# A two-layer graph attention network: column-split sums in layer 2, weights ahead of the rows, few in-edges first

## The chip, the cores and the metric

The kernel runs on one core of a Trainium2 chip. The metric is the device time of one execution in microseconds (us), and lower is better. Three executions of the kernel before took 6455.11, 6468.38 and 6469.05 us; the median is 6468.38.

## The reference, cut to what matters

There are N = 10000 nodes with 768 features each, and 170000 edges: 80000 random pairs in both directions and a self loop for each node; the reference then adds a second self loop. The edges come sorted by their target. Two graph attention (GAT) layers follow each other, each with a layer norm and a residual product, and a layer norm without scale ends the whole:

```python
def gat_conv(x, ei, W, a_src, a_dst, bias, heads, out_ch):
    xl = (x @ W).reshape(n, heads, out_ch)
    e = leaky_relu(alpha_src[src] + alpha_dst[dst], 0.2)   # alpha = sum of xl * a, per node and head
    alpha = softmax of e over the edges of one target      # with + 1e-16 in the divisor
    return segment_sum(xl[src] * alpha[:, :, None], dst) + bias

h1 = relu(layer_norm(gat_conv(x, heads=4, out_ch=256))) + x @ Wr1 + br1     # 768 -> 1024
h  = layer_norm(gat_conv(h1, heads=1, out_ch=768)) + h1 @ Wr2 + br2         # 1024 -> 768
out = layernorm(x + h)
```

All numbers are float32.

## The kernel before, in words

**Stages.** The first stage (to about 955 us of the span) computes `x @ W1` for 79 tiles of 128 nodes and writes `table1`, one row of 1032 numbers (4128 bytes) a node: 1024 features, then four source and four target logits. In the same time it sorts the nodes by their number of in-edges, most first, into `order` (79 columns of 128 nodes) and builds `slots`: for the tile t of the sorted order, `SLOTS[t]` columns of row numbers, one for the node itself and one for each in-edge a node of this tile can have, filled up with a row of zeros whose logits are a large negative number. `SLOTS` comes from `slot_counts`, at build time, from the numbers of nodes and edges alone: 42 for the first tile, then 28, 27 and so on down to 11, 1470 in all. If the input's degrees don't fit these counts, another, general path runs.

**Gathers and ring.** In both layers a tile's rows come one slot at a time: an indirect DMA, issued by GpSimd (POOL), fetches for each of 128 nodes the row of one in-edge into a slot of a ring in SBUF, which `Ring` holds; 28 slots of 1032 columns in layer 1, 40 of 770 in layer 2. `ring.fetch` (line 388) issues gathers as far ahead as the ring allows: after the row of slot q is used, that of q + 28 or q + 40 is asked for. So the ring's next gather waits for the engine that used the slot last.

**Layer 1, per tile** (`ordered_layer1`, from line 581). `logits` (409 to 417) forms the edge weights from the last columns of all the tile's rows, `normalised` (423 to 426) divides them by their sum. The first two rows (`ON_PE1`) are summed by TensorE (PE), which multiplies the row by a diagonal matrix of its weights; ScalarE (ACT) makes the diagonals. The other rows go to VectorE (DVE) in `weigh`: one row in three as four `scalar_tensor_tensor` of 256 columns (line 439: multiply by the head's weight and add), two in three are first multiplied in place on ScalarE (line 433) and then added by one operation of 1024 columns (line 435). The sum `acc` is in PSUM. While the rows of tile t are summed, tile t - 1 is finished: `deviation` and `scaled` make the layer norm, line 635 applies the relu and adds `x @ Wr1`, `columns` transposes h on TensorE, and a product with `W2` gives the row of `table2` that is scattered to memory by an indirect DMA on POOL; the transposed h is stored to `h1_d`. The schedule is written out by hand (`manual_schedule`): each engine takes its instructions in the order of the code, and `events` places the pieces of tile t - 1 after a given row of tile t. All products and the transposes of layer 1 take their PSUM tiles from `ps_big`, two buffers of two banks each, which lives through the whole kernel; `ps_acc` has two more.

**Layer 2, per tile** (`ordered_layer2`, from line 683). The same ring with rows of 768 columns and two logits. All rows are summed by VectorE, one `scalar_tensor_tensor` of 768 columns each (line 439), into one PSUM tile of two banks. TensorE computes the residual: line 740 adds x, gathered by POOL, with an identity product, line 742 adds `h1 @ Wr2` from `h1_d`, which SyncE (SP) loads. x and h1 of tile t + 2 are asked for at the end of tile t (line 763). The last layer norm ends on ScalarE (line 733), and POOL scatters the result (line 758).

**The first tile.** The tile of 42 slots has more rows than a ring holds. It goes through `attend_parts`: groups of rows with a running maximum, whose sums are scaled down when the maximum rises. It is the first in both layers, since the nodes of most in-edges come first. All other tiles are whole.

Of the kernel before, what the change touches and what calls it, by code (L numbers as in the profile page):

```python
# [33 lines left out]
P = 128  # L34
# [9 lines left out]
RING2 = 40  # L44
ON_PE1 = 2
# [8 lines left out]
def slot_counts(n_nodes, n_edges):  # L54
# [8 lines left out]
    for t in range(-(-n_nodes // P)):  # L63
        room = t * P if t else 0.002
        k = next((k for k, m in enumerate(tails) if m + 4.0 * math.sqrt(m) * (t > 0) <= room), DEGREES - 3)
        counts.append(min(k + 1, DEGREES - 2))
# [4 lines left out]
def gnn_kernel(ctx, tc, x, x_cols, src, dst, src_col, dst_col, W1, a_src1, a_dst1, b1, g1, be1, Wr1, br1,  # L71
# [13 lines left out]
    FIRST = [sum(SLOTS[:t]) for t in range(NT)]  # L85
# [12 lines left out]
    ps_big = ctx.enter_context(tc.tile_pool(name="ps_big", bufs=2, space=PSUM))  # L98
    ps_tr = None

    @contextmanager
    def psum_for_transposes():

        nonlocal ps_tr
        with tc.tile_pool(name="ps_tr", bufs=2, space=PSUM) as ps_tr:
            yield
# [8 lines left out]
    slots = consts.tile([P, FIRST[-1] + SLOTS[-1]], I32, name="slots")  # L115
# [29 lines left out]
    def product(aT, w, n):  # L145

        k = w.shape[1]
        p = ps_big.tile([P, 2 * BANK], F32, name="big")
        for c in range(0, n, BANK):
            e = min(n, c + BANK)  # L150
            for j in range(k):
                nc.tensor.matmul(p[:, c:e], aT[:, j, :], w[:, j, c:e], start=(j == 0), stop=(j == k - 1))  # L152
        return p
# [226 lines left out]
    class Ring:  # L380
# [6 lines left out]
        def fetch(self, upto):  # L387
            for q in range(self.issued, min(upto, FIRST[-1] + SLOTS[-1])):
# [38 lines left out]

    def weigh(acc, row, e, dh, first=None, shared=False):

        if shared:  # L430
            for h in range(e.shape[1]):
                s = slice(h * dh, (h + 1) * dh)
                nc.scalar.activation(row[:, s], row[:, s], AF.Copy, scale=e[:, h:h + 1])  # L433
# [8 lines left out]
    def attend_parts(small, ring, acc, h_, ad, bias, heads, dh, t):  # L442
# [6 lines left out]
        for lo, hi in zip(cuts, cuts[1:]):  # L449
# [13 lines left out]
            for q in range(lo, hi):  # L463
                weigh(acc, ring.slot(q), e[:, q - lo], dh, shared=heads > 1 and (q - lo) % 3)
# [3 lines left out]
    def deviation(small, a, n):  # L468

        k = -(-n // BANK)  # L470
        st = small.tile([P, k, 6], F32, name="st")
        for j in range(k):
            nc.vector.bn_stats(st[:, j, :], a[:, j * (n // k):(j + 1) * (n // k)])
# [6 lines left out]
    def scaled(to, a, n, mean_and_deviation, g, b):  # L480

        mean, inv = mean_and_deviation
        nc.vector.scalar_tensor_tensor(to, a[:, :n], mean, g, op0=OP.subtract, op1=OP.mult)
# [29 lines left out]
    with tc.tile_pool(name="w1", bufs=1) as w1p, tc.tile_pool(name="l1", bufs=2) as io, \  # L513
            psum_for_transposes(), tc.manual_schedule():
# [65 lines left out]

    def ordered_layer1():
        with tc.tile_pool(name="b1", bufs=1) as pool, tc.tile_pool(name="small1", bufs=2) as small, \
                tc.tile_pool(name="ps_acc1", bufs=2, space=PSUM) as ps_acc, tc.manual_schedule():
            ring = Ring(pool, table1, R1, RING1)
            ring.fetch(RING1)

            def fetch_x(t):
                xt = pool.tile([P, D0], F32, name="xt", bufs=2)
                gather(xt, x[:, :], order[:, t:t + 1])
                return xt  # L590

            xs = {t: fetch_x(t) for t in range(min(2, NT))}
            g1_b, be1_b = (spread(pool, v, n) for v, n in ((g1, "g1"), (be1, "be1")))

            def transposed_x(t):
                to = pool.tile([P, K0, P], F32, name="xT", bufs=2)
                return to, columns(to, xs[t])

            xT, moves = transposed_x(0)
            last = None  # L600
            for t in range(NT + 1):
                live, events = t < NT, []
                whole = live and SLOTS[t] <= ring.size
                n = SLOTS[t] if live else 0
                if live:
                    acc = ps_acc.tile([P, 2 * BANK], F32, name="acc")
                if whole:
                    ad = ring.slot(FIRST[t])[:, C1 + H1:]
                    e, _ = logits(small, ring, FIRST[t], FIRST[t] + n, ad, H1, C1)
                if last:  # L610
                    h, r, mean_rows = last
                    stats = deviation(small, mean_rows, C1)
                if whole:
                    normalised(small, e, H1)

                    diagonals = pool.tile([P, ON_PE1 * H1, P], F32, name="diagonals")
                    for k in range(ON_PE1):
                        for i in range(H1):
                            nc.scalar.activation(diagonals[:, k * H1 + i, :], ident, AF.Copy,  # L619
                                                 scale=e[:, k, i:i + 1])  # L620
                    for k in range(ON_PE1):
                        for i in range(H1):

                            c, d = i * DH1, (i + 1) * DH1
                            nc.tensor.matmul(acc[:, c:d], diagonals[:, k * H1 + i, :],  # L625
                                             ring.slot(FIRST[t] + k)[:, c:d],
                                             start=(k == 0 and c % BANK == 0),
                                             stop=(k == ON_PE1 - 1 and (d % BANK == 0 or d == C1)),
                                             skip_group_check=True)
# [404 lines left out]
```

## Time and profile before

| What | Kernel before |
|---|---|
| median of three executions | 6468.38 us (6455.11 to 6469.05) |
| profiled execution, own time | 6474.16 us |
| its span in the trace | 6472.3 us |
| granted TensorE clock, mean | 0.819 |
| VectorE busy | 5053.9 us (78% of the span) |
| TensorE busy, matmuls / weight loads | 4198.2 us (65%) / 2278.5 us |
| GpSimd busy | 3534.4 us (55%) |
| ScalarE busy | 2688.0 us (42%) |
| moved by DMA | 1666 MB, 257 GB/s in the mean |

An engine's busy time is that of its own instructions, without the time in which it waits for another. Lines such as L439 are line numbers of the kernel. A group of instructions is shown as line, engine, operation, output <- inputs, the shape of each, xcount, then busy time in us, the mean ns of one, and the idle time of the engine ahead of them with what ended it. In a timeline the first number is the time at which a run of instructions of one line starts, the second its length, and the square brackets hold the wait ahead of it.

### The profile page before, as it was taken

What the parts mean: (1) busy time and instruction counts of PE and PEld (TensorE: products, weight loads), DVE (VectorE), ACT (ScalarE), POOL (GpSimd) and SP (SyncE); (2) the same over time, 40 slices, a digit from 0 to 9 for tenths busy, and PEclk for the clock granted to TensorE, in tenths of its full rate; (3) what the DMA queues carried; (4) which work ended last, traced back from release to release, by engine and by line L of the source; (5) the groups of instructions that cost most, each with busy time, mean ns of one, the idle gap of its engine ahead of it and who ended that gap; (6) DMA issues with size and microseconds to landing.
All of it is one profiled execution on the core that took longest, in us unless ns stands there. A gap on an engine that the chain in (4) does not pass through costs nothing. (4 is left out here: it accounts for less than half of the span.)

```text
span 6472.3 us, 48744 instructions
## 1 busy us (share of the span) xinstructions
PE 4198.2 (65%) x11636; PEld 2278.5 (35%) x11636; DVE 5053.9 (78%) x8160; ACT 2688.0 (42%) x6591; POOL 3534.4 (55%) x3582
## 2 busy tenths in 40 slices
PE   8997982556766777778888996333434444445555
PEld 3443431333434444444455553111212222222332
DVE  5861426888888888888888884888878888888888
ACT  3433434666666666667666772011111111111111
POOL 3426534555555555555555553666666666666663
PEclk9999996778888888889899998666667777777777
DMA  4323237888888888888888885888878888888884
GB/s 140 122 76 70 93 106 287 289 293 315 299 301 301 303 304 297 300 295 299 293 299 307 308 312 180 277 281 288 281 272 287 282 280 281 279 286 283 279 291 161
DMA packets 459455, 1666.17 MB, mean 257 GB/s; under 512 B 105739, under 2 KB 109899, under 8 KB 459158
## 3 DMA queue, kind: packets, MB, share of 16 engines
q0 software_dynamic: 362176, 1486.59, 66.6%
q1 hardware_dynamic: 93168, 170.98, 7.8%
q10 hardware_dynamic: 3814, 5.39, 0.3%
q8 instruction: 94, 1.54, 0.1%
q14 instruction: 203, 1.66, 0.1%
HBM read 1516.88 MB, written 146.19 MB: 257 GB/s over the span
## 5 line engine op out<-in xcount | busy, mean ns | idle before, releaser
L364 POOL DMA_INDIRECT ring<-table,slots x2940 | 2789.2, 949 | 2161.4 <-DVE acc L439 889.7
L439 DVE SCALAR_TENSOR_TENSOR acc<-ring,e,acc 128x256 f32<-128x256 f32 (+1 forms) x3248 | 2332.4, 718 | 363.5 <-PE acc L625 201.5
L433 ACT ACTIVATE ring<-ring,e 128x256 f32<-128x256 f32 x3400 | 1390.8, 500 | 0.0
L435 DVE TENSOR_TENSOR acc<-acc,ring 128x1024 f32<-128x1024 f32 x850 | 1048.0, 1233 | 91.9 <-ACT ring L433 2.6
L740 PE MATMUL big<-wr,ident 128*128 128x512 f32 (+1 forms) x316 | 206.7, 745 | 1280.2 <-DMA wr<-in_x_dram,order 633.2
L742 PE MATMUL big<-w,wr 128*128 128x512 f32 (+1 forms) x2528 | 950.4, 531 | 23.1 <-issue 23.0
L625 PE MATMUL acc<-ring,diagonals 128*128 128x256 f32 x1248 | 424.3, 514 | 698.9 <-ACT diagonals L619 586.8
L152 PE MATMUL big<-w,hT 128*128 128x512 f32 (+1 forms) x2528 | 840.2, 490 | 56.8 <-ACT hT L494 56.8
L152 PE MATMUL big<-w,xT 128*128 128x512 f32 x1896 | 833.4, 601 | 55.8 <-DMA xT<-in_x_cols_dram 34.7
L152 PE MATMUL big<-wr,xT 128*128 128x512 f32 x1896 | 829.5, 594 | 0.7 <-ACT xT L494 0.7
L742 PEld LDWEIGHTS big<-w,wr 128*128 128x128 f32 x2528 | 531.3, 210 | 468.1 <-issue 432.6
L477 ACT ACTIVATE sd<-mv,eps 128x1 f32<-128x1 f32 x237 | 69.7, 294 | 1358.1 <-issue 585.4
L152 PEld LDWEIGHTS big<-w,hT 128*128 128x128 f32 x2528 | 471.9, 189 | 411.8 <-issue 289.1
L625 PEld LDWEIGHTS acc<-ring,diagonals 128*128 128x128 f32 x1248 | 326.9, 269 | 782.7 <-ACT diagonals L619 598.2
L152 PEld LDWEIGHTS big<-w,xT 128*128 128x128 f32 x1896 | 363.3, 193 | 522.9 <-issue 501.8
L740 PEld LDWEIGHTS big<-wr,ident 128*128 128x128 f32 x316 | 69.7, 249 | 1349.3 <-issue 449.3
L152 PEld LDWEIGHTS big<-wr,xT 128*128 128x128 f32 x1896 | 360.8, 190 | 423.4 <-issue 417.7
L417 ACT ACT_TABLE_LOAD x156 | 200.1, 1283 | 717.7 <-DVE e L416 636.7
L569 DVE TENSOR_TENSOR scr<-big,as_b 128x1024 f32<-128x1024 f32 x79 | 96.7, 1224 | 441.2 <-ACT row L566 426.3
L574 POOL TENSOR_TENSOR row<-row,none 128x1024 f32<-128x1024 f32 x79 | 187.0, 2368 | 334.9 <-ACT row L566 334.3
L572 ACT ACTIVATE scr<-scr 128x256 f32<-128x256 f32 x632 | 253.4, 402 | 122.2 <-DVE scr L569 118.3
L477 ACT ACT_TABLE_LOAD x157 | 201.4, 1283 | 229.7 <-DVE mv L475 149.5
(146 smaller groups left out, 3359.3 us busy)
## 6 DMA issues: line engine op xcount, KB each, us to landing
ring<-table,slots POOLq DMA_INDIRECT x2940
table<-row SPq DMA_DIRECT2D x79, 516.0 KB
h_d<-hT SPq DMA_DIRECT2D x79, 512.0 KB
wr<-h_d SPq DMA_DIRECT2D x79, 512.0 KB
xT<-in_x_cols_dram SPq DMA_DIRECT2D x79, 384.0 KB
w<-in_W_dram SPq DMA_DIRECT2D x6, 512.0 KB
w<-in_W_dram SPq DMA_DIRECT2D x1, 3072.0 KB
wr<-in_Wr_dram SPq DMA_DIRECT2D x1, 3072.0 KB
```

Of the source, the lines that this page charges most:

```text
L152: nc.tensor.matmul(p[:, c:e], aT[:, j, :], w[:, j, c:e], start=(j == 0), stop=(j == k - 1))
L364: nc.gpsimd.indirect_dma_start(out=to, out_offset=None, in_=table, in_offset=bass.IndirectOffsetOnAxis(ap=index, axis=0), **more)
L417: nc.scalar.activation(e, e, AF.Exp)
L433: nc.scalar.activation(row[:, s], row[:, s], AF.Copy, scale=e[:, h:h + 1])
L435: nc.vector.tensor_add(acc[:, :c], acc[:, :c], row[:, :c])
L439: nc.vector.scalar_tensor_tensor(acc[:, s], row[:, s], e[:, h:h + 1], (acc if first is None else first)[:, s], op0=OP.mult, op1=OP.add)
L477: nc.scalar.activation(sd, mv[:, 1:2], AF.Sqrt, bias=eps)
L572: nc.scalar.activation(m[:, s], m[:, s], AF.Copy, accum_out=row[:, C1 + i * H1 + h:C1 + i * H1 + h + 1])
L574: nc.gpsimd.tensor_add(row[:, :C1], row[:, :C1], b1_b)
L625: nc.tensor.matmul(acc[:, c:d], diagonals[:, k * H1 + i, :], ring.slot(FIRST[t] + k)[:, c:d], start=(k == 0 and c % BANK == 0), stop=(k == ...
L740: nc.tensor.matmul(r[:, c:d], ident, xt[:, c:d], start=True, stop=False)
L742: nc.tensor.matmul(r[:, c:d], hT[:, j, :], wr2[:, j, c:d], start=False, stop=(j == K1 - 1))
```

## The change

1. `slot_counts` takes the spread of a binomial count (the factor `1 - m / n_nodes`) for its margin; the counts are now 42, 28, ... 10, 9, in all 1456.
2. `SLOTS` and `FIRST` are turned around after the first stage and `nodes(t)` reads `order` from its end: tiles with few in-edges come first, that of 42 slots last.
3. Layer 1: `weights_of(t + 1)` makes the weights, the diagonals and TensorE's two rows of the next tile `LEAD` = 3 rows before the end of tile t. ScalarE's multiplies are issued three rows ahead of the row that is added, by `multiplied`. Three of four rows (`SHARE` = 4) are multiplied on ScalarE. The statistics of the layer norm and its square root (line 493 after) stand in front of the tile's multiplied rows. The transposes of x are made in the tile that uses them. The row of `table2` is copied and scattered one tile later, in `store`.
4. Layer 1's PSUM: one tile of `ps_h1` for transposes and the product with `W2`, one of `ps_r1` for `x @ Wr1`, two for the sums.
5. Layer 2: the columns 0 to 511 (`ON_PE2` = 512) are summed by VectorE as before, the columns 512 to 767 by TensorE with a diagonal for each row (`sums`), each in a PSUM tile of one bank of its own; ScalarE makes the diagonals. The bias of TensorE's columns comes by a product with ones. `deviation` and `scaled` take the two tiles as parts; the statistics are taken over three pieces of 256 columns.
6. Layer 2: the next tile's weights are made three rows ahead; x and h1 of the next tile are asked for at the middle row; the product with `br1` is made after the first tile's residual and added at the end of its rows. At the start of each layer the gathers of the first tile stand ahead of the first x, the rest of the ring after it.

The diff, cut; a helper's body that only moved is left out:

```diff
-        k = next((k for k, m in enumerate(tails) if m + 4.0 * math.sqrt(m) * (t > 0) <= room), DEGREES - 3)
+        k = next((k for k, m in enumerate(tails)
+                  if m + 4.0 * math.sqrt(m * (1.0 - m / n_nodes)) * (t > 0) <= room), DEGREES - 3)
...
+    FIRST = [sum(SLOTS[t + 1:]) for t in range(NT)]
...
+    def multiply(row, e, dh):
+        for h in range(e.shape[1]):
+            s = slice(h * dh, (h + 1) * dh)
+            nc.scalar.activation(row[:, s], row[:, s], AF.Copy, scale=e[:, h:h + 1])
...
+    def deviation(small, parts):
+        st = small.tile([P, len(parts), 6], F32, name="st")
+        for j, a in enumerate(parts):
+            nc.vector.bn_stats(st[:, j, :], a)
...
+    def scaled(to, parts, mean_and_deviation, g, b):
...
+        for a in parts:
+            d = c + a.shape[1]
+            nc.vector.scalar_tensor_tensor(to[:, c:d], a, mean, g[:, c:d], op0=OP.subtract, op1=OP.mult)
+            c = d
         nc.vector.reciprocal(inv, inv)
         nc.vector.scalar_tensor_tensor(to, to, inv, b, op0=OP.mult, op1=OP.add)
...
+    SLOTS, FIRST = SLOTS[::-1], FIRST[::-1]
+    def nodes(t):
+        return order[:, NT - 1 - t:NT - t]
...
     def ordered_layer1():
...
+                tc.tile_pool(name="ps_h1", bufs=1, space=PSUM) as ps_big, \
+                tc.tile_pool(name="ps_r1", bufs=1, space=PSUM) as ps_r, tc.manual_schedule():
...
+            def weights_of(t):
+                n = SLOTS[t]
+                e, _ = logits(small, ring, FIRST[t], FIRST[t] + n, ring.slot(FIRST[t])[:, C1 + H1:], H1, C1)
+                yield e
+                normalised(small, e, H1)
+                acc = ps_acc.tile([P, 2 * BANK], F32, name="acc")
...
+                yield acc
+            def shared(k):
+                return (k - ON_PE1) % SHARE > 0
...
+            def store(t):
+                nonlocal full
+                row = pool.tile([P, R2], F32, name="row")
+                nc.scalar.copy(row, full[:, :R2])
+                full = None
+                nc.gpsimd.indirect_dma_start(
+                    out=table2[:, :], out_offset=bass.IndirectOffsetOnAxis(ap=nodes(t), axis=0),
+                    in_=row, in_offset=None)
             for t in range(NT + 1):
...
                 if last:
+                    r, mean_rows = last
+                    stats = deviation(small, pieces(mean_rows[:, :C1], BANK))
+                if full is not None:
+                    store(t - 2)
...
+                    xT = pool.tile([P, K0, P], F32, name="xT")
+                    moves = columns(xT, xs[t])
+                multiplied(ON_PE1 + 2)
                 if last:
+                    h = pool.tile([P, C1], F32, name="h")
+                    scaled(h, [mean_rows[:, :C1]], stats, g1_b, be1_b)
+                    nc.vector.scalar_tensor_tensor(h, h, 0.0, r[:, :C1], op0=OP.max, op1=OP.add)
...
+                    events = [(ON_PE1 + j, move) for j, move in enumerate(columns(hT, h))]
+                if live:
+                    r = product(xT, wr1, C1, ps_r)
+                def to_layer2():
+                    nonlocal full
+                    nc.sync.dma_start(h1_d[t - 1], hT.rearrange("p k n -> p (k n)"))
+                    full = product(hT, w2, R2)
+                if last:
+                    events.append((ON_PE1 + 2, to_layer2))
...
+                for k in range(n if whole else 0):
+                    multiplied(k + 1 + LEAD)
+                    if k >= n - LEAD:
+                        ready += itertools.islice(ahead, 1)
+                    if k >= ON_PE1:
+                        weigh(acc, ring.slot(FIRST[t] + k), e[:, k], DH1, shared=shared(k))
+                    ring.fetch(FIRST[t] + k + 1 + ring.size)
+                    due(k)
...
     def ordered_layer2():
...
+                tc.tile_pool(name="ps_acc2", bufs=2, space=PSUM) as ps_acc, \
+                tc.tile_pool(name="ps_q2", bufs=2, space=PSUM) as ps_big, tc.manual_schedule():
...
+            def sums(t, acc, e):
+                n = SLOTS[t]
+                nc.tensor.matmul(acc, ones, b2_b[0:1, ON_PE2:], start=True, stop=False)
+                for k in range(n):
+                    if k == n // 2:
+                        yield
+                    if k % G == 0:
+                        diagonals = pool.tile([P, G, P], F32, name="diagonals", bufs=2)
+                    nc.scalar.activation(diagonals[:, k % G, :], ident, AF.Copy, scale=e[:, k, :])
+                    nc.tensor.matmul(acc, diagonals[:, k % G, :],
+                                     ring.slot(FIRST[t] + k)[:, ON_PE2:C2], start=False, stop=(k == n - 1))
...
                 if last:
+                    h, r, means = last
+                    stats = deviation(small, [a for m in means for a in pieces(m, C2 - ON_PE2)])
+                    next(tail, None)
+                    scaled(h, means, stats, g2_b, be2_b)
                     nc.vector.tensor_add(h, h, r[:, :C2])
+                    mean, inv = deviation(small, pieces(h, C2 // 2))
                     o = pool.tile([P, C2], F32, name="out")
+                for _ in tail:
+                    pass
...
                 if live:
+                    r = residual(t)
+                    if not t:
+                        q = product(brT, wr2, C2)
...
+                    for k in range(n if whole else 0):
+                        if k >= n - LEAD:
+                            ready += itertools.islice(ahead, 1)
+                        weigh(acc, ring.slot(FIRST[t] + k), e[:, k], ON_PE2, None if k else b2_b)
+                        ring.fetch(FIRST[t] + k + 1 + ring.size)
+                        if last and k == 1:
+                            finish()
+                        if not t and k == n - LEAD:
+                            nc.vector.tensor_add(be2_b, be2_b, q[:, :C2])
+                        if t + 1 < NT and k == n // 2:
+                            ins[t + 1] = fetch_x(t + 1)
...
-                if t + 2 < NT:
-                    ins[t + 2] = fetch_x(t + 2)
```

## The prediction, made before the changed kernel was run

> **What bounds the kernel now.** I read the page's slices first, then the busy time by stage, then the groups by shape, then the timeline of one tile in each layer. The page (busy tenths in 40 slices of 162 us):
>
> ```profile
> PE   8997982556766777778888996333434444445555
> DVE  5861426888888888888888884888878888888888
> PEclk9999996778888888889899998666667777777777
> ```
>
> Slices 1 to 6 are the first product, 7 to 24 are layer 1, from 25 on layer 2. VectorE (DVE) is near 0.87 in both layers and TensorE is not. By stage (columns: stretch, length, then busy us of PE, PEld, DVE, ACT, POOL, granted clock, DMA share, GB/s):
>
> ```profile
> 955.00:1091.00 136.00, 15.73 (x36) 7.42 (x36) 76.99 (x138) 46.97 (x118) 68.31 (x73) 0.54 0.80 293
> 1091.00:3919.00 2828.00, 2144.58 (x6609) 1259.38 (x6610) 2421.89 (x3805) 1919.96 (x4577) 1464.98 (x1553) 0.87 0.85 298
> 3919.00:4103.00 184.00, 81.72 (x240) 45.40 (x239) 81.70 (x122) 22.82 (x52) 83.54 (x87) 0.72 0.67 232
> 4103.00:6440.00 2337.00, 1088.83 (x2772) 586.16 (x2770) 1972.10 (x3072) 338.29 (x462) 1493.79 (x1541) 0.72 0.82 277
> ```
>
> The cuts are where the softmax weights of a tile are ready (line 426): 77 tiles of layer 1 take 2828 us, 77 of layer 2 take 2337. The first stage (955 us) is not touched. The groups by shape give the prices:
>
> ```profile
> L364 POOL DMA_INDIRECT ring<-table,slots x2940 | 2789.2, 949 | 2161.4 <-DVE acc L439 889.7 <-issue 478.9 <-PE acc L625 422.3
> L439 DVE SCALAR_TENSOR_TENSOR acc<-ring,e,acc 128x768 f32<-128x768 f32 x1392 | 1423.2, 1022 | 99.7 <-DVE acc L439 42.8 <-issue 11.3 <-remote 3.1
> L435 DVE TENSOR_TENSOR acc<-acc,ring 128x1024 f32<-128x1024 f32 x850 | 1048.0, 1233 | 91.9 <-ACT ring L433 2.6 <-DVE acc L435 0.9 <-DVE acc L439 0.5
> L439 DVE SCALAR_TENSOR_TENSOR acc<-ring,e,acc 128x256 f32<-128x256 f32 x1856 | 909.2, 490 | 263.9 <-PE acc L625 201.5
> ```
>
> The gathers wait mostly for slots that VectorE has not freed: VectorE leads, the transfers follow. One tile boundary of layer 1 in VectorE's timeline:
>
> ```profile
> 2431.22 1.22 DVE L635 SCALAR_TENSOR_TENSOR h<-h,big 128x1024 f32<-128x1024 f32 x1
> 2435.16 2.06 DVE L439 SCALAR_TENSOR_TENSOR acc<-ring,e,acc 128x256 f32<-128x256 f32 x4 [2.72 <-PE acc L625]
> 2437.33 2.57 DVE L435 TENSOR_TENSOR acc<-acc,ring 128x1024 f32<-128x1024 f32 x2
> ```
>
> VectorE sits 2.72 us until TensorE's two rows are there; the group above adds this up to 201.5. An unmultiplied row costs 2.06 + 0.11 = 2.17, a multiplied one 2.57 / 2 = 1.285. In layer 2 the same timeline has two speeds:
>
> ```profile
> 5197.08 0.21 DVE L475 BATCH_NORM_AGGREGATE mv<-st 128x2 f32<-128x12 f32 x1 [1.74 <-remote]
> 5201.97 1.02 DVE L485 SCALAR_TENSOR_TENSOR wr<-wr,sd,be 128x768 f32<-128x768 f32 x1 [2.40 <-remote]
> 5204.78 0.18 DVE L169 SCALAR_TENSOR_TENSOR e<-e 128x19 f32<-128x19 f32 x1 [0.53 <-DVE e L409]
> 5211.77 16.89 DVE L439 SCALAR_TENSOR_TENSOR acc<-ring,e,acc 128x768 f32<-128x768 f32 x16
> ```
>
> In the last line a row takes 16.89 / 16 = 1.055. In the first three VectorE waits for nothing but itself and starts late. Summed over the stage these pauses are some 300 us, 3.9 a tile; tiles of 19 rows take 27.3 us without and 36 to 37 with them. I can't name their cause. POOL and TensorE in the same tile:
>
> ```profile
> 5214.75 0.95 POOL L364 DMA_INDIRECT ring<-table,slots  x1 [0.30 <-issue]
> 5216.00 0.95 POOL L364 DMA_INDIRECT ring<-table,slots  x1 [0.31 <-DVE acc L439]
> ```
>
> ```profile
> 5208.65 8.63 PE L742 MATMUL big<-w,wr 128*128 128x512 f32 x16
> 5217.55 3.62 PE L742 MATMUL big<-w,wr 128*128 128x256 f32 x16
> ```
>
> A gather comes every 1.25 us at best. A pass of 256 columns takes 0.226 us (3.62 / 16), one of 512 takes 0.43 once warm and 0.86 in the first five microseconds.
>
> **What the Trainium skill says.** "VectorE: DVE Perf Modes", section on the TRN2 errata: a fixed cost per instruction and then a slope by element. The trace agrees: 490 ns at 256 columns, 1022 at 768, so 1.04 ns a column. "DMA: Bandwidth & Descriptors", section "SWDGE vs HWDGE vs iDMA": descriptors of GpSimd's transfers are computed there in software; the trace has 0.95 + 0.30 us for each gather. "TensorE: Matmul & The Clock Gate", Part 1: half clock after idling; the 0.86 and 0.43 agree. "PSUM — Partial Sum Buffer", section on bank collisions: two engines must not be in one bank at once, so TensorE's 256 columns need a bank of their own; no run here shows a collision.
>
> **The change, part by part.** *Layer 1, rows.* Before, 77 tiles have 446 rows by VectorE alone and 817 multiplied on ScalarE: 446 x 2.17 + 817 x 1.285 = 2018, which leaves (2828 - 2018) / 77 = 10.5 a tile. After (three of four rows multiplied, 1456 slots instead of 1470 in each layer) 78 tiles have 344 and 914: 1921. ScalarE gets 914 x 4 x 0.41 = 1499 us of multiplies for 1346, some 28 us a tile with its copies and tables, under VectorE's 32 for 18 rows: hidden, with four to spare.
>
> *Layer 1, weights ahead.* The next tile's weights, diagonals and two TensorE rows are issued with three rows left, so the 2.7 goes: 7.8 a tile, 78 x 7.8 = 608, sum 2529. The square root now stands before the multiplied rows, which costs nothing: ScalarE runs ahead of VectorE. Three things are late next. TensorE needs 10.5 (24 passes at 0.436) + 10.6 (16 at 0.436, 16 at 0.226) + 3.6 (16 at 0.226) + 1.9 for transposes = 26.6 a tile, and now its transposes and the layer 2 product share one PSUM tile; tiles of 9 to 14 rows fall to that floor: +40. The weights want all rows of the next tile three rows earlier in a ring of 28; in the 16 tiles of 22 rows or more VectorE will wait for a gather, between 0 and 5 us each; I take 2.5: +40. The transfers must run at 11.0 MB in 33 us, 333 GB/s, where streaming windows show 340 to 356; between 0 and 1.5 us a tile, I take 0.5: +40. Layer 1's whole tiles: 2650 for 2828 + 23 (last tile).
>
> *Layer 2, columns.* 256 of 768 columns go to TensorE. A row of 512 is half way between 490 and 1022, 756, with its gap 0.79 instead of 1.055; at 19 rows this saves 5.0 of 27.3, and one more statistic and one more piece of the scaling give back 0.4. Average 22.1, with the old pauses 26.0. ScalarE gets 1414 diagonals at 0.386, 7 us a tile where it was idle. TensorE gets 36 passes at 0.226, 8.3, beside the 11.9 of the residual product: 20, hidden under VectorE if warm. A slot is now freed by both engines, but TensorE's share stands at the tile's start. The pace passes to POOL: 1414 x 1.253 + 78 x 2.6 (the x gather and the output scatter) = 1975, 25.3 a tile. The x gather moves to mid-tile, behind n/2 gathers and ahead of the rest, and the h1 load with it: TensorE's waits for x (633 us) had cover, now they go. I take 26.0 + 0.9 where neither covers the other, 26.9 x 78 = 2098 for 2337 + 13.
>
> *Order.* The 42-row tile is now last. Layer 1 starts after 9 gathers: 21 us instead of 136, but the large tile costs 64.6 in rows, 20 in group starts, fading and dividing and 6 for the tile ahead: 90. From layer 1's last row (3942) to layer 2's first whole tile (4103) passed 161, among it 39 of VectorE waiting for a bias and 32 for a product; now 22 (h, product, scatter) + 34 (9 gathers, bias): 56. At the end 57 for the large tile. Last 20 us as before.
>
> Sum: 955 + 21 + 2650 + 90 + 56 + 2098 + 57 + 20 = 5947, against 955 + 136 + 2828 + 23 + 161 + 2337 + 13 + 20 = 6473 (span 6472.3, its own time 6474.2, median 6468.4). Forecast 5950.
>
> **The rivals.** *B, pauses set layer 2's pace.* In a paused stretch VectorE's rows start every 1.40 us, and a 512 column row would too, so the saving is lost there; with POOL running without a break, stretches may grow. For it: pauses come late in long POOL runs and end when the gathers are through. Against: layer 1 has none. Layer 2 stays at 30.3 a tile: 78 x 30.3 = 2363, total 6215. *C, all cover holds:* layer 1 at 2569, layer 2 at POOL's 1975, total 5745. *D, slower:* TensorE becomes layer 2's bound. The new passes wait for a diagonal each; if the clock stays at half, a tile needs 18 x 0.86 + 18 x 0.43 + 37 x 0.43 = 39 us, 3042 in all, total 6890. It decides from 33.5 us a tile, the point where the gains elsewhere are eaten. Against it: layer 1 holds full clock at 19.3 of 20 us busy; for it: layer 2's clock is 0.72 today. That the input no longer fits the smaller slot counts, and the general path runs, I exclude: by the input's own in-degrees every tile of 128 nodes stays within its count.
>
> **How the numbers follow.** Forecast 0.52 (5850 to 6080), B 0.26 (6080 to 6350), C 0.13 (5700 to 5850), D 0.07, no difference 0.02. A run of this kernel tells 0.2% from nothing. Faster by more 0.91, within 0.02, slower 0.07. From 5790 to 6290 the range leaves out D, no difference, the top of B (0.03) and half of C: about 0.19.
>
> **What would show it.** Layer 1: no wait of VectorE for TensorE at line 449 in tiles over 15 rows, 33 to 34 us a tile; if it waits for ring gathers at line 415, the transfers bound it. Layer 2: gathers back to back at 1.25 with VectorE waiting at line 415; rows at 0.79; if rows start every 1.40, B. TensorE near 20 us a tile at a clock above 0.85; if VectorE waits at line 504 or 835 for a square root behind diagonals, D. The middle: layer 2's first tile some 56 us after layer 1's last row. A longer first stage would make the whole working wrong.

## The result and the profile after

On the chip of the record the changed kernel takes 6426.99 us (median of five runs, 6419.05 to 6432.44) and the kernel before 6455.39 us (median of five, the three above among them): a ratio of 0.995, 95% interval 0.9933 to 0.9967. It is faster by half a per cent where 8% was forecast.

The runs were made on several occasions, each on one chip; on some the kernel before took 6447 to 6482 us in all of its runs and on the others 6167 to 6172 us, so I call the first kind *late* and the second *in time*, for a reason that the traces give, and compare times within one kind only; the record is of the late kind, both kernels.

The changed kernel on record by stage; columns: stretch, length, then busy us of TensorE, its weight loads, VectorE, ScalarE and GpSimd, granted clock, DMA share, GB/s. The cuts are the first weights of layer 1, the start of its 42-row tile, the first weights of layer 2, and the start of its 42-row tile.

```profile
981.00:3645.00 2664.00, 2135.27 (x6674) 1238.34 (x6674) 2350.36 (x3504) 2080.63 (x4977) 1534.54 (x1580) 0.91 0.89 322
3645.00:3794.00 149.00, 40.32 (x106) 21.76 (x106) 80.38 (x136) 57.10 (x136) 42.70 (x44) 0.63 0.49 170
3794.00:6346.00 2552.00, 1894.23 (x5834) 1230.24 (x5835) 1614.14 (x3237) 757.04 (x1877) 1526.61 (x1583) 0.83 0.77 261
6346.00:6417.00 71.00, 7.48 (x25) 4.50 (x23) 55.34 (x88) 6.26 (x11) 5.26 (x4) 0.57 0.07 23
```

In layer 1 VectorE is busy 88% of the time (2350 of 2664 us). In layer 2 no engine is: VectorE has 63%, GpSimd 60%, TensorE 74%. The forecast had 2098 us where the third line has 2552. The groups of the same run show where VectorE stands (busy, mean ns, idle time ahead and what ended it):

```profile
L449 DVE SCALAR_TENSOR_TENSOR acc<-ring,e,acc 128x512 f32<-128x512 f32 x1336 | 1008.3, 755 | 39.4
L828 DVE TENSOR_TENSOR wr<-wr,big 128x768 f32<-128x768 f32 x79 | 75.4, 954 | 769.4 <-remote 555.7 <-PE sum L792 204.7 <-issue 8.8
```

A row of 512 columns costs 755 ns, as estimated. The idle time has one place: line 828, the addition of TensorE's residual, stands 769.4 us, 9.9 a tile. VectorE, then the queue of SyncE, GpSimd and ScalarE around one such wait:

```profile
5029.67 1.02 DVE L505 SCALAR_TENSOR_TENSOR wr<-wr,sd,be 128x768 f32<-128x768 f32 x1
5041.18 0.95 DVE L828 TENSOR_TENSOR wr<-wr,big 128x768 f32<-128x768 f32 x1 [10.49 <-remote]
```

```profile
5041.17 0.32 SPq L765 DMA_DIRECT2D wr<-h_d  x1
```

```profile
5036.81 1.03 POOL L871 DMA_INDIRECT out_dram<-out,order  x1 [0.30 <-issue]
5044.80 0.97 POOL L370 DMA_INDIRECT ring<-table,slots  x1 [6.96 <-DVE acc L449]
```

```profile
5041.39 0.40 ACT L791 ACTIVATE diagonals<-ident,e 128x128 f32<-128x128 f32 x1 [10.33 <-remote]
```

VectorE's addition, SyncE's load of h1 and ScalarE's ninth diagonal wait for matmuls that the trace has long behind them: the residual's last one starts at 5029.39, the sixth sum, past the four whose diagonals ScalarE overwrites, at 5032.80. All three go on within 0.22 us, 3.3 us after GpSimd's run of gathers and the scatter ended (5037.84). That is when the last packets of the run land, here at 5041.11: over layer 2 of this run the last packet of a transfer ends 3.2 us after GpSimd's instruction in the median, 2.8 to 3.6 in nine of ten.

What they share is TensorE's semaphore: SyncE's load and ScalarE's diagonal wait for nothing else, and VectorE's step that waits for its own semaphore ahead of the addition was through at 5030.75. The trace also notes when a semaphore was raised (us; the first two lines list the starts of TensorE's matmuls that raise it, by line, the third the times at which it was raised):

```
5017.78 L792  5020.14 L803  5023.57 L803  5026.37 L803  5027.23 L803  5028.10 L803  5028.96 L803  5029.39 L803
5030.02 L785  5030.64 ... 5032.80 L792 (6)  5038.14 L792
5040.93 5040.99 5041.05 5041.11 5041.16 5041.20 5041.24 5041.28 5041.33 5041.37 5041.41 5041.45 5041.50
```

Sixteen matmuls raise it, at least 0.43 us apart; from 5017.74 to 5040.93 no signal is noted, and then thirteen come in 0.57 us (three are missing from the trace). So TensorE had computed; its signals came late, all at once, when the gathers were through. The Trainium skill's "Perfetto Trace Analysis", section "Per-engine timelines", shows for each engine that a profiled instruction ends before its raised semaphore is seen everywhere, and that TensorE's end is an estimate. Here that remainder is 11.4 us for the residual's last matmul (5029.77 to 5041.18) and 8.2 us for the sixth sum (5033.18 to 5041.39).

A tile of layer 2 is then a closed round: VectorE waits at line 828 for the end of GpSimd's run; the first slot of the next tile comes free 3.6 us later (5041.18 to 5044.80); GpSimd issues 20 gathers and scatters at 1.25 us (to 5037.84), and 3.3 us later the addition goes on. 3.6 + 25.1 + 3.3 = 32.0, the time from one addition to the next (5009.14 to 5041.18).

On an occasion in time the same program takes 5926.08 us, beside 6169.19 for the kernel before: 0.961, one run of each, without an interval. Its stages, with the corresponding cuts, and the same group:

```profile
983.00:3636.00 2653.00, 2139.33 (x6675) 1239.21 (x6676) 2350.22 (x3504) 2080.61 (x4977) 1533.57 (x1580) 0.91 0.90 324
3636.00:3785.00 149.00, 38.68 (x106) 21.17 (x106) 80.25 (x134) 57.11 (x136) 41.99 (x45) 0.63 0.49 171
3785.00:5837.00 2052.00, 1733.64 (x5831) 1179.42 (x5832) 1620.05 (x3239) 764.62 (x1877) 1554.20 (x1576) 0.90 0.93 323
```

```profile
L828 DVE TENSOR_TENSOR wr<-wr,big 128x768 f32<-128x768 f32 x79 | 75.4, 954 | 11.4 <-PE big L803 3.5
```

Layer 1 is the same within 11 us. Layer 2 is 500 us shorter, the wait at line 828 is 11.4 us in all instead of 769.4, and GpSimd issues almost without a break. The granted clock of layer 2 is lower on the late occasion (0.83 for 0.90), but that does not explain the wait: in the tile above the residual's matmuls were through 11 us before the addition began. VectorE and GpSimd at one boundary of a tile there:

```profile
5124.26 1.02 DVE L505 SCALAR_TENSOR_TENSOR wr<-wr,sd,be 128x768 f32<-128x768 f32 x1
5125.39 0.95 DVE L828 TENSOR_TENSOR wr<-wr,big 128x768 f32<-128x768 f32 x1
```

```profile
5123.67 0.95 POOL L370 DMA_INDIRECT ring<-table,slots  x1 [0.30 <-issue]
5124.92 1.18 POOL L370 DMA_INDIRECT ring<-table,slots  x1 [0.30 <-PE sum L792]
5126.41 0.95 POOL L370 DMA_INDIRECT ring<-table,slots  x1 [0.30 <-DVE wr L828]
```

### The profile page after: what moved, and what is told of

The parts are those of the page before. It is cut to its first block, busy times and chain, and to the rows that moved or that the text cites. A ratio compares the mean times of both kernels' runs of the same rounds, so it can differ in the third digit from the quotient of the medians.

```text
span 6417.3 us, 57909 instructions
## 1 busy us (share of the span) xinstructions
PE 4943.3 (77%) x14620; PEld 2874.9 (45%) x14620; DVE 4584.9 (71%) x7969; ACT 3257.0 (51%) x8379; POOL 3547.9 (55%) x3554
## 5 line engine op out<-in xcount | busy, mean ns | idle before, releaser
L449 DVE SCALAR_TENSOR_TENSOR acc<-ring,e,acc 128x256 f32<-128x256 f32 (+1 forms) x2760 | 1705.2, 618 | 123.8 <-PE acc L641 37.7
L438 ACT ACTIVATE ring<-ring,e 128x256 f32<-128x256 f32 x3776 | 1532.8, 505 | 0.0
L792 PE MATMUL sum<-ring,diagonals 128*128 128x256 f32 x2828 | 914.5, 477 | 619.5 <-issue 327.7
L445 DVE TENSOR_TENSOR acc<-acc,ring 128x1024 f32<-128x1024 f32 x944 | 1163.0, 1232 | 93.1 <-issue 8.6
L792 PEld LDWEIGHTS sum<-ring,diagonals 128*128 128x128 f32 x2828 | 664.2, 241 | 866.8 <-issue 440.3
L803 PE MATMUL big<-w,wr 128*128 128x512 f32 (+1 forms) x2528 | 850.6, 488 | 29.8 <-issue 29.8
L791 ACT ACTIVATE diagonals<-ident,e 128x128 f32<-128x128 f32 x1414 | 441.9, 387 | 571.8 <-remote 384.8
L641 PE MATMUL acc<-ring,diagonals 128*128 128x256 f32 x1248 | 357.5, 450 | 380.3 <-ACT diagonals L636 346.3
L803 PEld LDWEIGHTS big<-w,wr 128*128 128x128 f32 x2528 | 479.7, 190 | 373.8 <-issue 340.0
L828 DVE TENSOR_TENSOR wr<-wr,big 128x768 f32<-128x768 f32 x79 | 75.4, 954 | 769.4 <-remote 555.7
```

Source lines behind the costliest of these rows:

```text
L445: nc.vector.tensor_add(acc[:, :c], acc[:, :c], row[:, :c])
L449: nc.vector.scalar_tensor_tensor(acc[:, s], row[:, s], e[:, h:h + 1], (acc if first is None else first)[:, s], op0=OP.mult, op1=OP.add)
L641: nc.tensor.matmul(acc[:, c:d], diagonals[:, k * H1 + i, :], ring.slot(FIRST[t] + k)[:, c:d], start=(k == 0 and c % BANK == 0), stop=(k == ...
L791: nc.scalar.activation(diagonals[:, k % G, :], ident, AF.Copy, scale=e[:, k, :])
L792: nc.tensor.matmul(acc, diagonals[:, k % G, :], ring.slot(FIRST[t] + k)[:, ON_PE2:C2], start=False, stop=(k == n - 1))
L803: nc.tensor.matmul(r[:, c:d], hT[:, j, :], wr2[:, j, c:d], start=False, stop=(j == K1 - 1))
```

## The experiments

All edits are made in the changed kernel. *Theory J*: on some occasions the signals of gathers at full rate hold up those of the engines, TensorE's above all. *Theory K*: VectorE waits at line 828 for the end of the run of gathers by the order of the program.

**Columns back on VectorE**, in time first, late second; the sums on TensorE, its diagonals and the second PSUM tile go:

```diff
-                    acc = ps_acc.tile([P, BANK], F32, name="acc")
-                    sum_ = ps_acc.tile([P, BANK], F32, name="sum")[:, :C2 - ON_PE2]
-                    tail = sums(t, sum_, e)
+                    acc = ps_acc.tile([P, 2 * BANK], F32, name="acc")[:, :C2]
...
-                        weigh(acc, ring.slot(FIRST[t] + k), e[:, k], ON_PE2, None if k else b2_b)
+                        weigh(acc, ring.slot(FIRST[t] + k), e[:, k], DH2, None if k else b2_b)
```

> The changed kernel with layer 2's columns put back: all 768 on VectorE, no diagonals and no sums on TensorE. Theory J (TensorE's signals pile up behind those of a run of gathers; the more matmuls TensorE signals, the longer VectorE waits for them at the residual's addition, 10 us a tile now): 27 signals a tile are left of about 47, the wait shrinks and a whole tile of layer 2 takes some 30.3 us, as before, instead of 32.3: about 6250. Rival K (VectorE waits there for the end of POOL's run of gathers, whatever TensorE does): the tile stays at POOL's run and the round trip, 32.3: about 6417.

It took 5954.6 us, with the kernel before at 6172.45: lower than both expectations, because this occasion was in time and I had assumed a late one. Three more edits ran beside it:

> The changed kernel with one small memset on GpSimd after each gather of layer 2, so that a gather comes every 1.5 us or so instead of every 1.25. Theory J: signals no longer pile up, the 10 us wait falls under 2 and GpSimd's 20.4 x 1.5 = 30.6 sets the tile: about 6290. Rival K: the wait lasts until the longer run is through, 20.4 x 1.5 + 6.6 = 37.2 a tile: about 6795.

> The changed kernel with gathers of layer 2 of 616 bytes a row instead of 3080, as many of them; the rows are not those of the reference, the weights neither, and the ring is cleared once (some 30 us). Theory J (it is the number of signals): the wait stays and the tile stays at 31 to 32.3: 6350 to 6450. Rival M (it is the bytes that fill the way into SBUF): the wait goes, GpSimd's 25.5 sets the tile: about 5930.

> The changed kernel without h1 @ Wr2 in the residual of layer 2: only x by the identity, 3 matmuls a tile instead of 27; part of the computation is left out. Theory J: TensorE's signals fall from about 47 to 23 a tile, the wait at the residual's addition falls under 3 us and the tile comes to 26 or 27: about 6000. Rival K: still 32.3, about 6417.

They took 6176.13, 5934.48 and 5948.48 us. Without late signals there was nothing for these three to separate; the kernel before, 283 us under its time on record, was the finding. That is the size of the pauses of "some 300 us" that the prediction read from its trace; no trace of the kernel before was taken in time, so that they are the same 300 us is not shown. The changed and the earlier kernel themselves came next, with the columns once more:

> The changed kernel itself, unedited, beside the three edits of it, because the kernel before took 6172 us on the chip of the first four runs and 6455 to 6469 on the one of the record. Theory J (late signals): if this chip gives the kernel before in 6170, the changed kernel has no 10 us wait at the residual's addition either and takes about 5950 to 6000; if it gives 6460, the wait is there and it takes about 6420. Theory K (the wait is in the order of the program): about 6420 on either chip.

> The kernel before, unedited, for its trace on this chip. Theory J: where it takes 6170, the 300 us in which VectorE waits for nothing but itself in layer 2 are gone, and the rest of its stages stands as on record. Theory K: the pauses are there in any trace.

> Layer 2's columns back on VectorE, on the same chip as the changed kernel: VectorE's rows then set a tile at 26.5, about 5955 on a chip without late signals. Against the changed kernel on the same chip it tells what the columns alone are worth: theory J says nothing or less than 1% without late signals (GpSimd's 25.5 a tile is near), and 150 to 250 us in favour of this kernel with them; K says 150 to 250 us in favour of this kernel on any chip.

The occasion was late: 6457.4 us for the kernel before (median of seven; 6453.34 in its traced run), 6429.92 for the changed kernel (0.9954, 0.9938 to 0.9971), 6236.17 without the columns (0.9653, 0.9636 to 0.9669). The columns alone cost 194 us there. In the trace without them the addition (then line 826) waits 66.7 us in all:

```profile
L826 DVE TENSOR_TENSOR wr<-wr,big 128x768 f32<-128x768 f32 x79 | 75.4, 954 | 66.7 <-remote 44.0 <-PE big L803 8.7 <-PE big L801 6.8
```

The changed kernel was run again:

> The changed kernel once more. If this chip gives the kernel before in about 6170: theory J (late signals, found only on the chip with 6455) says 5950 to 6000 with no long wait at the residual's addition; theory K (order of the program) says about 6420. If it gives it in about 6455, 6420 to 6435 as known.

> The changed kernel with the memset on GpSimd after each gather of layer 2 (a gather every 1.58 us instead of 1.25, 29.3 a tile on the first chip, 6176 in all), on whichever chip this is. On a chip with 6455 for the kernel before: theory J (the signals of a run of gathers at full rate hold up those of TensorE) says that at this rate they don't, the wait at the residual's addition falls under 2 us and the time is 6180 to 6250. Theory K (the wait lasts until the run of gathers is through, at any rate): about 6750.

This occasion was in time, and the two took 5926.08 and 6178.69 us. So the wait is not in the order of the program, and K in that form falls. In time the columns gain little: 0.961 of the kernel before with them, 0.965 without (5954.6 of 6172.45), single runs on two occasions.

**What goes with late signals: gathers of 616 bytes a row, and slower gathers.** The gathers of layer 2 read a fifth of a row, in the same number; the rows and weights are then not the reference's.

```diff
-                gather(self.slot(q), self.table[:, :], slots[:, q:q + 1])
+                gather(self.slot(q)[:, :self.part],
+                       self.table.rearrange("n (a b) -> (n a) b", b=self.part), slots[:, q:q + 1])
...
             ring = Ring(pool, table2, R2, RING2)
+            ring.part = 154
+            nc.vector.memset(ring.rows, 0.0)
```

> The changed kernel with gathers of 616 bytes a row in layer 2 for 3080 (the rows and weights are then not the reference's, and the ring is cleared once). On a chip with 6170 for the kernel before it took 5934. On one with 6455: theory J in its narrow form (the number of signals alone) says 6350 to 6450 as before; theory M (signals are held up by the bytes of the gathers on their way) says about 5950.

Late occasion (6470.74 for the kernel before): 6448.75 us, and the group of the addition:

```profile
L832 DVE TENSOR_TENSOR wr<-wr,big 128x768 f32<-128x768 f32 x79 | 75.4, 954 | 709.6 <-remote 390.4 <-PE sum L796 274.3 <-PE big L807 23.6
```

The wait stays with a fifth of the bytes in as many gathers, so theory M, that the bytes hold the signals up, falls. The rate was then changed, with a memset on GpSimd after each gather:

```diff
                 gather(self.slot(q), self.table[:, :], slots[:, q:q + 1])
+                if self.pace is not None:
+                    nc.gpsimd.memset(self.pace, 0.0)
```

> The changed kernel with a smaller memset on GpSimd (128 columns for 256) after each gather of layer 2: a gather every 1.45 us. On a chip with 6170 for the kernel before: GpSimd sets the tile, about 27.5, some 6050. On one with 6455: theory J (the signals of gathers at full rate hold up those of TensorE) says that 16 per 1.45 us is near what layer 1 sends without harm (9.65 a us against 11), so that most of the wait at the residual's addition goes: 6050 to 6150. Theory K (the wait lasts until the run of gathers is through): 6590.

> The changed kernel with the memset of 256 columns after each gather of layer 2: one every 1.58 us. With 1.45 us the wait at the residual's addition stayed at 9 us a tile on a chip with 6470 for the kernel before. On such a chip: theory J with a threshold of rate (10.1 signals of gathers a us is what layer 1 sends without such waits) says the wait falls under 3 us: 6200 to 6280. Theory K (any run of gathers holds TensorE's signals up until it ends, at any rate): the run is 2.7 us longer and the tile too, 6550 to 6650. On a chip with 6170: 6176 as before.

> The changed kernel with a memset of 512 columns on GpSimd after each gather of layer 2: one every 1.9 us, 8.4 signals of gathers a us, fewer than layer 1 sends (9.65). On a chip with 6455 for the kernel before: theory J (rate) says the wait at the residual's addition is under 2 us a tile and GpSimd sets the tile at 18.3 x 1.9 + 2.6 = 37.4, about 6810. Theory K (a run of gathers holds TensorE's signals up at any rate): GpSimd's run and the round trip of 6.6, 44 a tile, about 7320. On a chip with 6170: 6810.

The first was late: 6404.8 us, a gather every 1.34 us (0.95 + 0.22 + 0.17, since the gap ahead of a gather is 0.17 after a memset, not 0.30; my 1.45 was wrong), and the addition waits 713.5 us:

```profile
L832 DVE TENSOR_TENSOR wr<-wr,big 128x768 f32<-128x768 f32 x79 | 75.4, 954 | 713.5 <-remote 574.4 <-PE sum L796 113.1 <-PE sum L789 22.3
```

The second fell on an occasion in time (6174.91, 6167.56 for the kernel before) and says nothing here; its memset of 256 columns takes 0.33 us and gives a gather every 1.45 us, not the 1.58 of the expectations, and layer 1 sends 9.65 signals a us, not 10.1. The third was late (6472.88 for the kernel before) and took 6487.53 us. Its memset and its addition:

```profile
L398 POOL MEMSET pace<- 128x512 f32 x1456 | 788.2, 541 | 0.7
L832 DVE TENSOR_TENSOR wr<-wr,big 128x768 f32<-128x768 f32 x79 | 75.4, 954 | 20.0 <-PE big L807 12.0
```

A gather comes every 1.65 us (0.95 + 0.54 + 0.17), 0.25 less than I had expected, and the wait is gone, from 769.4 to 20.0. The time is GpSimd's now, and so 6487.53 us is no gain. The rate decides, as J says, between 1.34 and 1.65 us a gather, by one run of each on two late occasions.

With a slower GpSimd the rows, and with them the addition, come later, and that alone could have hidden the wait. It is not so: in the middle of layer 2 of the changed kernel on record, 50% of the matmuls that raise TensorE's semaphore have no rise noted within 1 us of their end; 42% with a fifth of the bytes, 48% at 1.34 us, 3% at 1.65 us, and none in time.

The traces count it. A gather has 16 packets of 4 bytes; in time each answers to one noted rise of a DMA semaphore, so I take them for its signals. Per us, in the middle of layer 1 and in layer 2 without its edges:

```
kernel, occasion                      layer 1: sent  noted    layer 2: sent  noted
changed, in time                                9.65   9.65             12.36  12.35
changed, late (record)                          9.64   6.98             10.00   1.97
before, late (record)                           8.85   7.52             10.74   1.89
changed, fifth of the bytes, late               9.65   6.50              9.94   1.40
changed, gather every 1.34 us, late             9.65   6.45             10.07   2.83
changed, gather every 1.65 us, late             9.65   6.36              9.74   8.63
```

In time all signals are noted at any rate. On late occasions 72 to 86% of layer 2's are missing from the trace at full rate and at 1.34 us, though the data lands, and at 1.65 us most are back. A missing note is not a late signal by itself: from 5027.00 to 5042.15 none of VectorE's own is noted in the tile above, and its wait for them was through at 5030.75. Every execution, of both kinds, was recorded with its span and clock; whether the recording takes part in the delay was not tried. Sent is an average over runs at full rate (16 per 1.25 us = 12.8) and the breaks between them.

**TensorE's share**, h1 @ Wr2 left out of the residual:

```diff
-                    nc.tensor.matmul(r[:, c:d], ident, xt[:, c:d], start=True, stop=False)
-                    for j in range(K1):
-                        nc.tensor.matmul(r[:, c:d], hT[:, j, :], wr2[:, j, c:d], start=False,
-                                         stop=(j == K1 - 1))
+                    nc.tensor.matmul(r[:, c:d], ident, xt[:, c:d], start=True, stop=True)
```

> The changed kernel without h1 @ Wr2 in layer 2 (part of the computation is left out), 3 matmuls a tile for 27. On a chip with 6170 for the kernel before it took 5948. On one with 6455: theory J says TensorE has 23 signals a tile to get through for 47 and the wait at the residual's addition falls from 10 us to under 4: 6000 to 6150. Theory K: 6420.

> Layer 2's columns on VectorE and no h1 @ Wr2 (left out): 3 matmuls of TensorE a tile. On a chip with 6455 for the kernel before: a tile of layer 2 took 32.3 us with about 47 of TensorE's signals, 29.9 with 27, 29.7 with 23. Theory J (TensorE's signals add up with those of the gathers): about 27, 6000 to 6060. If TensorE's count doesn't matter beside VectorE's own: 29.5, about 6210. On a chip with 6170: 26.5 a tile, about 5955.

Late, the first took 6225.75 us, above J's 6000 to 6150 and below K's 6420. The addition waits 38.1 us in all, but VectorE then stands elsewhere: 134 us at its rows (52 of them for its own signal by the trace), 122 at line 429 and 117 at 832 for ScalarE's, 93 at 489 for TensorE's sums. The expectation's numbers were off: the trace has 25 raises of TensorE's semaphore a tile in the changed kernel, 20 here and 7 with the columns on VectorE, not 47, 23 and 27. With 5 fewer the wait left the addition, so their number alone does not explain it; that the residual ends earlier may. The second fell on an occasion in time (5974.59). Number and moment of TensorE's signals are not told apart.

**The place of the waiting instruction.** The addition and the statistics after it stand at row 6 of the next tile, the last scaling at row 8:

```diff
-                    nc.vector.tensor_add(h, h, r[:, :C2])
-                    mean, inv = deviation(small, pieces(h, C2 // 2))
...
-                        if last and k == 1:
+                        if last and k == 6:
+                            add()
+                        if last and k == 8:
                             finish()
```

> The changed kernel with the residual's addition and the statistics after it at row 6 of the next tile instead of ahead of its first row, and the last scaling at row 8. On a chip with 6455 for the kernel before: theory J says VectorE still waits there until POOL's queue is empty, but rows have been summed by then and the next slots come free 1 us after the wait, not 3.6: 2 to 3 us a tile less, 6200 to 6280. If the wait were for TensorE's residual itself, it would be gone: 5950. On a chip with 6170: within 20 us of 5926.

> The residual's addition at row 6 of the next tile, timed against the kernel before. On a chip with 6170 for the kernel before it took 5891 (the changed kernel 5926): 0.955 of the kernel before. On one with 6455: theory J says VectorE still waits there until GpSimd's queue is empty but loses 2 to 3 us less a tile: 6200 to 6280, 0.965.

In time it took 5890.94 us (6167.56 for the kernel before), 35 less than the changed kernel on another occasion in time. Late it took 6341.7 us (0.979, 0.9771 to 0.9809): better than 0.995, but not the 6200 to 6280 expected. The addition waits 112.8 us, and 331 have moved to VectorE's wait for ScalarE at the last scaling (line 840) and 250 to its wait for TensorE's sums (line 489): other instructions need late signals too.

**Both edits**, the columns on VectorE and the addition at row 6:

> The changed kernel with layer 2's columns back on VectorE and the residual's addition at row 6 of the next tile. If the kernel before takes about 6170 (signals in time): VectorE's rows set the tile at 26.5, about 5950, 0.965 of the kernel before. If it takes about 6460 (late signals): VectorE waits for fewer of TensorE's signals than with the columns and later in the tile, 6150 to 6236, 0.955 to 0.965, and the columns are what cost the changed kernel its gain there. If the place of the addition alone mattered, it would stay near the 0.979 that this edit gave with the columns.

The occasion was in time: 5921.56 us (0.960, 0.9584 to 0.9616), 28 us under the estimate. Whether this version is the best on a late occasion was not tried; of the complete kernels that ran there, the changed kernel without the columns is the best (0.9653).

## Why the prediction was wrong

The sum's terms, in us. The forecast was made against a late occasion, so the record is the column that counts.

| Term | Forecast | Record (late) | In time |
|---|---|---|---|
| first gathers of layer 1 | 21 | 26 | 28 |
| layer 1, 78 whole tiles | 2650 | 2664 | 2653 |
| 42-row tile and middle | 90 + 56 | 149 | 149 |
| layer 2, 78 whole tiles | 2098 | 2552 | 2052 |
| 42-row tile and end | 57 + 20 | 71 | 87 |
| with the first stage, 955 | 5947 | 6417 | 5924 |

**Right: layer 1, the order, the middle.** The three costs that were taken for layer 1 (small tiles at TensorE's floor, late gathers in large ones, transfers) come out at 2664 for 2650 as a sum. Two of them are there in the trace at their size: VectorE waits 37.7 us for TensorE's rows (line 449) in 13 of the first 14 tiles, for 40, and 45.3 us for gathers (line 415) in 15 larger ones, for 40. The third, 40 for the transfers, shows as no wait of its own, while 36.1 us stand at line 429 for ScalarE's exponential, which the sum did not have; that these two nearly cancel is luck. Tiles of 18 rows take 32.2 to 32.6 us, under the 33 to 34 of the text. VectorE's wait for TensorE's rows was 201.5 us before. The large tile took 79 and the middle 70, for 90 and 56.

**Wrong: "The pace passes to POOL" and "26.9" in layer 2.** The working put the unexplained pauses in the average that the columns bring down (22.1, "with the old pauses 26.0") and let GpSimd's 25.3 cover them. In the changed kernel the pauses are not idle time of VectorE's own that another engine can cover: they are late signals while GpSimd gathers at full rate, and they stop the loop that feeds GpSimd. (That those of the kernel before have the same cause rests on the missing signals of its trace and on the 283 us.) The columns put TensorE's matmuls for the next tile's first rows and the late end of the residual into that run; VectorE waits for them ahead of its first row, frees no slot, and GpSimd runs dry once a tile. So the cover failed, and the term is 2552, 32.7 a tile for 26.9. In time, where there are no late signals, the same step is right: 2052 for 2098, gathers back to back at 1.25 us, rows at 0.79, TensorE's clock 0.90, though TensorE is busy 22.2 us a tile (1734 / 78) and not 20.

**Rival B had the direction, not the form or the size.** It priced the pauses at 30.3 a tile, with rows every 1.40 us, total 6215. The rows run at 0.79; the pause stands in one instruction and is 9.9 us a tile, more than the 3.9 before. B's pauses had the size of those in the kernel before, and the range ended at 6290. That a pause without a known cause could grow with the edit needed a wider range: the text itself said "stretches may grow", and it had seen that pauses come late in GpSimd's long runs and end when the gathers are through, but no term of the sum used it.

**Rivals C and D.** D did not come: TensorE was not the bound, and the clock was 0.83 late and 0.90 in time. C's 1975 for layer 2 was missed by 77 us even in time: there GpSimd's instructions take 1554 us and their gaps of 0.30 some 473, 2027 in all, since a gather takes 0.982 us in the mean and not 0.95. VectorE waits 154 us at line 429 for ScalarE's exponential and 144 at line 415 for gathers.

Where the gain went, by the two traces on record: from 955 us to the last row of layer 1 the kernel before takes 2987 us (to 3942) and the changed one 2769 (to 3724), 218 gained. From there to the end they take 2530 and 2693, 163 lost. The rest, 55, is the difference of the spans (6472.3 and 6417.3). The runs agree: late, without the columns the changed kernel has 3.5% (0.9653), and the columns take 194 us of it back.

## What to carry to other kernels

A pause that a profile shows and that no instruction explains is no fixed cost: find which signals come late and during which work before moving a wait under it. Where one engine feeds another through a ring, an instruction that waits on a third engine should stand behind the first rows that free slots, not ahead of them. And an edit that gains in one place can be judged only where the machine's condition is that of the profile: time the kernel before beside it each time.

## What the runs showed of the hardware

- On some occasions signals come late while GpSimd issues gathers at full rate, and on others not, for the same program: 6447 to 6482 us against 6167 to 6172 for the kernel before. It is not the chip's listed number: one number appeared under both conditions. The cause stays open.
- It goes with the rate of the gathers (gone at one in 1.65 us, there at 1.34 and 1.25), not with their bytes (616 or 3080 a row): VectorE waits 20, 714, 769 and, with 616 bytes, 710 us at one addition. The signals then come at once: 13 of TensorE's in 0.57 us. Whether TensorE's wait longer than the other engines', and why, is open.
- A memset on GpSimd between two gathers shortens the gap ahead of the next one from 0.30 to 0.17 us, so a memset of 0.22 us costs 0.09.
